# When the first gathered blocks are made: four raw blocks during the load of x, nine beside the terms of the table, and the loop's first loads behind the table's stores

## The chip, the core and the metric

The kernel runs on one core of one Trainium2 chip. The metric is the device time of one execution in microseconds (us). Before the change it is 2218.24 us, the median of 10 runs between 2216.36 and 2223.97.

A core has several engines that run side by side and wait for each other through semaphores: PE multiplies matrices (its weight loads have a row of their own in the profile, PEld), DVE works on vectors element by element, ACT applies functions and copies, POOL is the general engine, which here issues the gathers, and SP issues most other transfers. Transfers are done by 16 DMA engines. [...]

## The reference

One layer of a graph network on 12,500 nodes of 128 features and 212,500 edges that are sorted by their destination `dst`:

```python
h = jnp.maximum(_layernorm(x, axis=-1), 0.0)
q = h @ Wq.T + bq            # per node, 8 heads of 16
v = h @ Wv.T + bv            # per node
k = edge_attr @ Wk.T + bk    # per edge
in_m   = sum(q[src] * k)     # per edge and head
out_m  = sum(q[dst] * k)
diag_m = sum(q[src] * q[dst])
score = (softmax over the edges of each dst of in_m/4, + of out_m/4, + of diag_m/4)
score = score * edge_weight ** lam       # lam = 1
out = x + leaky_relu(segment_sum(score * v[dst]) @ Wo.T + bo)
```

For the change one thing matters: each edge needs the row `q[src]` of an arbitrary node. That row must be gathered, and before it can be gathered from a table the table has to be there.

## The kernel before

**Tiling.** The edges are cut into 415 groups of 512 (four tiles of 128 edges each). Five streams `s` run through the sorted edges at once, 83 blocks `t` each; group `g` is block `g // 5` of stream `g % 5`. The nodes are handled in 25 turns (`GN`) of up to four tiles of 128 nodes.

**The node stage.** A turn normalises its node tiles (statistics on DVE at L869 to L880, the root on ACT at L884, its inverse on DVE at L888 and L889), rectifies them (ACT, L898), turns them with PE and copies the result (L905, L907), multiplies by Wq (L913), adds the bias on DVE (L916) and stores the rows of q to the table `q_table` in memory (SP, L917). The turns are software-pipelined: turn `g` issues the product of its own tiles, the turn of the next and the rectifying of the one after that.

**Gathers.** `gather(g)` issues four indirect transfers on POOL (L683), each of which fetches 128 rows. It cannot take rows from `q_table` before the last of the table is stored. So that POOL need not stand still, the first 13 groups (`RAW`) are gathered from `x` itself; they are called raw blocks. For a raw block the kernel then has to do what a node turn does, on the gathered rows: `raw_measure` (DVE, L957), the sums of a set of up to three blocks, `raw_root` (ACT) and `raw_invert` (DVE), and per block `raw_rectify` (ACT, L972), `raw_turn` (PE L978, ACT L980), `raw_product` (PE L985) and `raw_add` (DVE L989). From group 13 on rows come from `q_table`.

**What sets the order.** Every instruction is pinned in the order in which the program issues it. Between the node turns, `aside(turn)` issues whatever the dictionary `side` holds for that turn; the places are written out by hand. In the kernel before, raw blocks are measured in turns 5 to 7, 12 to 14, 17 to 19, 22, 23, 25 and 26, and block `g` is rectified in turn `9 + 2 * g` for the first seven, in turn `GN + g - 7` for the six others. The dictionary also holds the preparation of the edge tables: casts of the indices to floats (POOL), `edges_1` (POOL, L821), `edges_3` and `edges_5` (DVE), `cuts` (ACT, L835), and `edges_4`, which stores the tables `far_d` and `rel_d` (SP).

**The terms.** For the windows of destination nodes the table also exists as three bf16 terms per value. For the 8 first node turns that the loop needs, `terms_q` makes them after the node stage, in 9 iterations (ACT L933 and L940, DVE L934 and L941), and SP stores them (L943). The raw blocks that are left stand beside these iterations.

**Loads ahead.** `fetch(t)` loads two edge tables of block `t` (`relb`, 630 KB by the profile, L648; `far`, L653) and reads the first node of each window from `places`; `fetch_rows(t)` loads the windows `win` (L665); `fetch_edges(t)` loads 1280 KB of edge features `ea` (L671). `when` (POOL) makes a ruler of expected first nodes, and `near_due` (DVE, L806 to L811) corrects it by the true ones, which gives `places`.

**The loop.** Group `g` of the loop does: products of the window with a one-hot matrix (PE L1224, ACT L1227), the turn and projection of the edge features (PE L1207, L1214, L1216, ACT L1209), three products and a sum on DVE (L1235 to L1238), the one-hot of group `g + 3` (ACT L1201, L1202), and the softmax work of earlier blocks. In iteration `g`, `gather(g + 18)` is held behind PE's products of group `g`, one tile's gather behind each of four places (`behind`). Ahead of the loop 21 groups are gathered. In the first five iterations ACT also issues a large store of blanks each (L1649, 1056 to 1152 KB).

Of the kernel before, what the change touches and what calls it, by code (L numbers as in the profile page):

```python
# [7 lines left out]
F32 = mybir.dt.float32  # L8
# [464 lines left out]
def ordered_path(ctx: ExitStack, tc: tile.TileContext, flag, x, src, dst, edge_attr, edge_weight,  # L473
# [19 lines left out]
    nc = tc.nc  # L493
# [7 lines left out]
    S = 5  # L501
    T = (NB + S - 1) // S
# [17 lines left out]
    START, RATE, NEAR = round(G * BE * N / E), BE * N // E, 90  # L520
# [20 lines left out]
    GN = -(-NI // JN)  # L541
    in_use = sorted((first_use(g), g) for g in range(GN))
    early = [g for t, g in in_use if t < 4]
# [13 lines left out]
    def pin(inst):  # L557

        engine = str(inst.ins.engine)
        if engine in pinned:  # L560
            tc.add_manual_dep(inst.ins, pinned[engine], mybir.DependencyInfo(
                mybir.DependencyClass.NoSync, mybir.DependencyReason.DATA), reason="in order")
        pinned[engine] = inst.ins.name
        return inst
# [15 lines left out]
                   allow_small_or_imprecise_dtypes=True))  # L580
# [29 lines left out]
    bases = consts.tile([1, T, S], I32, name="bases")  # L610
    tops = consts.tile([1, T, S], I32, name="tops")
    heads = consts.tile([1, T, S], I32, name="heads")
    LOOK, QQ, RAW, DRAIN = 18, 20, 13, 12
# [7 lines left out]
    places = consts.tile([1, T, S], I32, name="places")  # L621
# [14 lines left out]
    def block_rows(t):  # L636
        lo = t if t < G else t - 1
        return lo, slice(0, S * G) if t < G else slice(1, S * G + 1)

    def fetch(t):  # L640

        if t >= T:
            return
        at, part = block_rows(t)
        relb = None
        if t < G:
            relb = load.tile([K3, S, BE], BF, name="relb")
            pin(nc.sync.dma_start(relb, rel_d[part].rearrange("(s b) e -> s b e", b=G)  # L648
                                  [None, :, at, :].to_broadcast([K3, S, BE])))
        far = load.tile([R, BE + 1], BF, name="far", bufs=4)  # L650
        lo = t * BE
        of = bass.AP(far_d.tensor, far_d.offset + lo, [[G * BE, S], [0, H3], [1, BE + 1]])
        pin(nc.sync.dma_start(far, of))  # L653
        _, base_v[t] = nc.values_load_multi_w_load_instructions(
            places[0:1, t, 0:S], engines=[mybir.EngineType.SP], min_val=0, max_val=N - 1,
            skip_runtime_bounds_check_because="the indices of nodes are below N")
        st[t] = dict(relb=relb, far=far)
# [10 lines left out]
    def fetch_edges(t):  # L668
        if t < G:
            ea = eas[t] = load.tile([P, S, JN * F], F32, name="ea")  # L670
            pin(nc.sync.dma_start(  # L671
                ea, edge_attr[:end * BE, :].rearrange("(s b p j) f -> p s b (j f)", s=S, b=G, p=P)
                [:, :, t, :]))
# [50 lines left out]
    with tc.tile_pool(name="prep", bufs=1) as prep, \  # L724
# [73 lines left out]
        def of_tile():  # L798
            return prep.tile([P, RC], BF, name="of", tag="of", bufs=2)[:RW]

        def when():
            pin(nc.gpsimd.iota(places, pattern=[[RATE, T], [START, S]], base=0, channel_multiplier=0))

        def near_due():
            offset = prep.tile([1, T, S], F32, name="offset", tag="terms")
            pin(nc.vector.tensor_sub(offset, bases, places))  # L806
            pin(nc.vector.tensor_reduce(found[:, 4:5], offset, AX.XY, ALU.min))
            pin(nc.vector.tensor_reduce(found[:, 5:6], offset, AX.XY, ALU.max))
            pin(nc.vector.tensor_scalar(offset, offset, -float(NEAR), float(NEAR), op0=ALU.max,
                                        op1=ALU.min))  # L810
            pin(nc.vector.tensor_add(places, places, offset))  # L811

        def cast_src():
            pin(nc.gpsimd.tensor_copy(src_f, src_r))
# [78 lines left out]
        def tiles_of(g):  # L893
            return range(g * JN, min(NI, (g + 1) * JN))

        def rectify(g):
            for i in tiles_of(g):
                pin(nc.scalar.activation(xq[:, i, :], xq[:, i, :], AF.Relu, bias=shift[:, i:i + 1],  # L898
                                         scale=inv[:, i:i + 1]))

        def turn_h(g):
            n = len(tiles_of(g))
            h_ps = node_ps.tile([P, JN, P], F32, name="h_ps")
            for b, i in enumerate(tiles_of(g)):
                pin(nc.tensor.transpose(h_ps[:, b, :], xq[:, i, :], ident))  # L905
            hT = hTs[g] = node.tile([P, JN, P], F32, name="hT", bufs=2)
            pin(nc.scalar.copy(hT[:, :n], h_ps[:, :n]))  # L907

        def nodes_q(g):
            n = len(tiles_of(g))  # L910
            q_ps = node_ps.tile([P, JN, F], F32, name="q_ps")
            for b in range(n):
                pin(nc.tensor.matmul(q_ps[:, b, :], hTs[g][:, b, :], wq, start=(b == 0),  # L913
                                     stop=(b == n - 1)))
            q = xq[:, g * JN:g * JN + n, :]
            pin(nc.vector.tensor_add(q, q_ps[:, :n], bq_all[:, None, :].to_broadcast([P, n, F])))  # L916
            pin(nc.sync.dma_start(units(q_table, g * 2, n // 2, F),  # L917
                                  q.rearrange("p (u k) f -> p u (k f)", k=2)))
            del hTs[g]
# [3 lines left out]
        def terms_q(i):  # L923

            if i < len(early):
                g = early[i]
                n = len(tiles_of(g))
                q = xq[:, g * JN:g * JN + n, :]
                q3 = (node.tile([P, JN, 3, F], BF, name="q3", bufs=1) if i % 4 == 1 else
                      prep.tile([P, JN, 3, F], BF, name="q3w", tag="weight") if i % 4 == 0 else  # L930
                      prep.tile([P, JN, 3, F], BF, name="q3o", tag="of", bufs=2))
                q3 = q3s[g] = q3[:, :n]
                pin(nc.scalar.copy(q3[:, :, 0, :], q))  # L933
                pin(nc.vector.tensor_sub(q, q, q3[:, :, 0, :]))  # L934
            if i > 0:
                g = early[i - 1]
                n = len(tiles_of(g))
                q = xq[:, g * JN:g * JN + n, :]
                q3 = q3s.pop(g)
                pin(nc.scalar.copy(q3[:, :, 1, :], q))  # L940
                pin(nc.vector.tensor_sub(q3[:, :, 2, :], q, q3[:, :, 1, :]))  # L941
                lo = g * JN * P
                pin(nc.sync.dma_start(  # L943
                    q3_table[3 * lo:3 * (lo + n * P), :].rearrange("(u p k) f -> p u (k f)", p=P, k=6),
                    q3.rearrange("p (u k) t f -> p u (k t f)", k=2)))
# [48 lines left out]
        def turn_att(a):  # L994
            turn_edges(weight, att_t, [a])

        side = {4: [turn_ws], 5: [cast_src, (gather, 7), cast_dst, (gather, 8)],
                10: [(turn_src, 0)], 11: [(turn_src, 1)], 12: [(turn_src, 2)],
                13: [(turn_src, 3), when, edges_1] + [(gather, g) for g in range(9, RAW)],
                14: [biases], 20: [near_due], 15: [edges_3], 16: [(turn_att, 0), cuts], 17: [(turn_att, 1)],  # L1000
                18: [(turn_att, 2), edges_4], 19: [(turn_att, 3)], 21: [edges_5], 22: [(fetch, 0)]}

        def raw_side(lo, hi, turns):
            for g, turn in zip(range(lo, hi), turns):
                side.setdefault(turn, []).append((raw_measure, lo, hi, g))
            side[turn].append(raw_root)
            side.setdefault(turn + 1, []).append(raw_invert)

        raw_side(0, 3, (5, 6, 7))
        raw_side(3, 6, (12, 13, 14))  # L1010
        raw_side(6, 9, (17, 18, 19))
        raw_side(9, 11, (22, 23))
        raw_side(11, RAW, (GN, GN + 1))
        for g in range(RAW):
            turn = 9 + 2 * g if g < 7 else GN + g - 7
            for k, f in enumerate((raw_rectify, raw_turn, raw_product, raw_add)):
                side.setdefault(turn + k, []).append((f, g))

# [20 lines left out]
        def settle():  # L1039

            while rooted:
                invert(*rooted.pop(0))
# [8 lines left out]
        for g in range(-2, GN):  # L1051
            settle()
            if g + 2 < GN:
                rectify(g + 2)
            if 0 <= g + 1 < GN:
                turn_h(g + 1)
            if g >= 0:
                nodes_q(g)
            ready(g + 4)
            measure(g + 6 + min(max(g, 0), 6))  # L1060
            if g == -2:
                for of in range(7):
                    gather(of)
            aside(g)
            if g == 9:
                fetch_edges(0)
                fetch_few()
        for g in range(RAW, AHEAD):
            gather(g)
        gather_few()  # L1070
        for i in range(len(early) + 1):
            terms_q(i)
            aside(GN + i)
        assert not side

# [115 lines left out]
    with tc.tile_pool(name="work", bufs=2) as work, \  # L1191
# [383 lines left out]

        products = str(mybir.EngineType.PE)
        fetch_rows(0)
        fetch(1)
        fetch_rows(1)
        one_hots(0)  # L1580
        turn(0)
# [168 lines left out]
```

## Time and profile before

| | |
|---|---|
| median of 10 runs | 2218.24 us |
| profiled execution | 2217.78 us |
| its span | 2215.7 us |
| PE busy | 1728.3 us (78%) |
| DVE busy | 2043.0 us (92%) |
| ACT busy | 1369.8 us (62%) |
| POOL busy | 1608.7 us (73%), of it the gathers 1542.3 us |
| first gather from the table | 106.88 us |
| last gather | 2144.56 us |

Starts are in us from the start of the span. A row of the timeline gives the start, the busy time, the engine, the line of the kernel, the operation, what it writes and reads, and in brackets how long the engine was idle before and what ended this. The name of the engine with a q (ACTq, SPq) marks the issue of a transfer, which is not counted as busy. PEclk is the clock that PE was granted, as a share of full speed. A row of the waits gives the engine and its instruction, what it waited for, the sum in us, how often, and the longest. The share of busy time is an average over stages with different limits, so it is read stage by stage. POOL's gathers count as busy for 0.95 us but start 1.26 us apart when nothing holds them, the rest being the issue.

### The profile page before, as it was taken

What the parts mean: (1) busy time and instruction counts of PE and PEld (TensorE: products, weight loads), DVE (VectorE), ACT (ScalarE), POOL (GpSimd) and SP (SyncE); (2) the same over time, 40 slices, a digit from 0 to 9 for tenths busy, and PEclk for the clock granted to TensorE, in tenths of its full rate; (3) what the DMA queues carried; (4) which work ended last, traced back from release to release, by engine and by line L of the source; (5) the groups of instructions that cost most, each with busy time, mean ns of one, the idle gap of its engine ahead of it and who ended that gap; (6) DMA issues with size and microseconds to landing.
All of it is one profiled execution on the core that took longest, in us unless ns stands there. A gap on an engine that the chain in (4) does not pass through costs nothing.

```text
span 2215.7 us, 36271 instructions
## 1 busy us (share of the span) xinstructions
PE 1728.3 (78%) x10744; PEld 1362.6 (61%) x10744; DVE 2043.0 (92%) x2837; ACT 1369.8 (62%) x2517; POOL 1608.7 (73%) x1683
## 2 busy tenths in 40 slices
PE   6767777777777778888878888887888777778775
PEld 4545656665656666666766666665666665556654
DVE  8768999999999999999999999999999999999894
ACT  6756566566666666666666665666666655566661
POOL 7377777777777777777777777777777777777750
PEclk9977888889798888887787888779888988888786
DMA  7676545545555555555455555555455455454531
GB/s 212 199 244 186 162 148 163 181 151 173 168 156 156 178 177 166 154 163 170 141 175 157 150 169 159 147 166 158 150 165 160 149 153 165 149 149 141 159 95 58
DMA packets 321411, 355.65 MB, mean 161 GB/s; under 512 B 135266, under 2 KB 241005, under 8 KB 320896
## 3 DMA queue, kind: packets, MB, share of 16 engines
q1 hardware_dynamic: 250853, 237.91, 34.0%
q0 software_dynamic: 53184, 108.92, 17.3%
q10 hardware_dynamic: 17168, 6.41, 1.2%
q8 instruction: 88, 1.44, 0.3%
q14 instruction: 118, 0.97, 0.1%
HBM read 320.86 MB, written 32.17 MB: 159 GB/s over the span
## 4 chain that ended last, share of the span: by engine, by line
DVE 32%; PE 24%; DMA 21%; ACT 9%; issue 9%; POOL 4%; SPq 0%; DVEq 0%; ACTq 0%; POOLq 0%
DMA qq<-q_table,src_i 20%; DVE lT L1238 10%; PE k_ps L1216 8%; DVE prod L1236 5%; DVE prod L1235 5%; DVE prod L1237 5%; PE w_ps L1388 4%; POOL qq L683 4%; PE eT_ps L1207 3%; PE k_ps L1214 2%; DVE l_ps L1298 2%; PE qd_ps L1224 2%; PE node_ps L1147 1%; ACT relb L1201 1%; ACT eT L1209 1%
## 5 line engine op out<-in xcount | busy, mean ns | idle before, releaser
L683 POOL DMA_INDIRECT qq<-q_table,src_i x1608 | 1542.3, 959 | 513.6 <-issue 220.8
L1238 DVE TENSOR_REDUCE lT<-prod 128x96 f32<-128x1536 f32 x415 | 727.4, 1753 | 14.3
L1216 PEld LDWEIGHTS k_ps<-wk,eT 128*128 128x128 f32 x3320 | 500.9, 231 | 170.7 <-issue 75.9
L1216 PE MATMUL k_ps<-wk,eT 128*128 128x128 f32 x3320 | 593.9, 333 | 12.0 <-ACT eT L1209 11.7
L1209 ACT COPY eT<-eT_ps 128x512 f32<-128x512 f32 x415 | 243.4, 587 | 392.5 <-PE eT_ps L1207 382.2
L1224 PE MATMUL qd_ps<-win,oh 126*128 126x128 bf16 x1660 | 183.0, 240 | 297.8 <-DVE prod L1236 290.4
L1224 PEld LDWEIGHTS <-oh 126*128 126x128 bf16 x1660 | 136.6, 107 | 359.8 <-issue 338.4
L1227 ACT COPY qd<-qd_ps 128x512 f32<-128x512 f32 x415 | 239.3, 577 | 131.4 <-PE qd_ps L1224 109.5
L1207 PE MATMUL eT_ps<-ident,ea 128*128 128x128 f32 x1660 | 311.2, 321 | 2.9 <-DVE qq L989 2.9
L1201 ACT ACTIVATE relb<-relb,before 126x512 bf16<-126x512 bf16 x415 | 301.1, 726 | 0.0
L1236 DVE TENSOR_TENSOR prod<-qq,qd_ps 128x512 f32<-128x512 f32 x412 | 279.9, 679 | 22.9 <-DMA qq<-q_table,src_i 18.7
L1235 DVE TENSOR_TENSOR prod<-qd,k_ps 128x512 f32<-128x512 f32 x415 | 279.5, 673 | 22.1 <-ACT qd L1227 9.2
L1237 DVE TENSOR_TENSOR prod<-qq,k_ps 128x512 f32<-128x512 f32 x412 | 279.6, 679 | 0.0
L1202 ACT ACTIVATE oh<-relb 126x512 bf16<-126x512 bf16 x415 | 261.3, 630 | 16.9 <-DMA q_table<-q3o 3.7
L1207 PEld LDWEIGHTS eT_ps<-ident,ea 128*128 128x128 f32 x1660 | 249.3, 170 | 3.1 <-DVE qq L989 3.1
L1388 PE MATMUL w_ps<-back,sel 128*126 128x144 f32 (+1 forms) x1344 | 207.4, 314 | 44.8 <-ACT sel L1378 37.7
L1388 PEld LDWEIGHTS w_ps<-back,sel 128*126 128x126 f32 (+1 forms) x1344 | 193.9, 211 | 58.4 <-ACT sel L1378 50.3
L1214 PE MATMUL k_ps<-b,ones 3*128 3x512 bf16 x415 | 180.4, 435 | 29.0 <-DVE prod L1237 24.1
L1349 ACT ACTIVATE back<-back 128x480 f32<-128x480 f32 x83 | 50.1, 604 | 190.9 <-DVE back L1348 187.5
L1298 DVE TENSOR_TENSOR_SCAN l_ps<-far,carry,l_ps 120x512 f32<-120x512 bf16 x80 | 102.4, 1280 | 5.2 <-PE l_ps L1258 5.2
L1328 DVE TENSOR_TENSOR_SCAN m<-far,head,l_ps 120x512 f32<-120x512 bf16 x81 | 102.9, 1271 | 0.0
L1340 PE MATMUL m_ps<-ident,m 120*128 120x120 f32 x332 | 77.1, 378 | 24.9 <-DVE m L1328 24.1
(230 smaller groups left out, 1611.3 us busy)
## 6 DMA issues: line engine op xcount, KB each, us to landing
ea<-in_edge_attr_dram SPq DMA_DIRECT2D x83, 1280.0 KB
relb<-rel_d SPq DMA_DIRECT2D x83, 630.0 KB
qq<-q_table,src_i POOLq DMA_INDIRECT x1608
win<-q_table SPq DMA_DIRECT2D x415, 31.5 KB
far<-far_d SPq DMA_DIRECT2D x84, 120.2 KB
q_table<-q SPq DMA_DIRECT2D x18, 384.0 KB
sums<-rows SPq DMA_DIRECT2D x412, 7.9 KB
q_table<-xq SPq DMA_DIRECT2D x24, 256.0 KB
```

The costliest lines, as they stand in the source:

```text
L683: rows = pin(nc.gpsimd.indirect_dma_start(out=qq[:, j, :], out_offset=None, in_=of, in_offset=bass.IndirectOffsetOnAxis(ap=at[:, s, j:j + ...
L1201: pin(nc.scalar.activation(d, d, AF.Abs, bias=before[:K3]))
L1202: pin(nc.scalar.activation(oh, d, AF.Relu, bias=1.0, scale=-1.0))
L1207: pin(nc.tensor.transpose(eT_ps[:, j, :], eas[g // S][:, g % S, j * F:(j + 1) * F], ident))
L1209: pin(nc.scalar.copy(eT, eT_ps))
L1216: pin(nc.tensor.matmul(k_ps[:, j, :], eTs[g][:, j, :], wk, start=False, stop=(j == JN - 1)))
L1224: pin(nc.tensor.matmul(qd_ps[:, j, :], ohs[g][:, j * P:(j + 1) * P], d["win"][:, s, :], start=(j == 0), stop=(j == JN - 1)))
L1235: pin(nc.vector.tensor_mul(prod[:, :, 2, :], qds[g], ks[g]))
L1236: pin(nc.vector.tensor_mul(prod[:, :, 1, :], qqs[g], q_ps[g]))
L1237: pin(nc.vector.tensor_mul(prod[:, :, 0, :], qqs[g], ks[g]))
L1238: pin(nc.vector.tensor_reduce(lTs[t][:, :, s, :], prod.rearrange("p j i (h d) -> p j (i h) d", d=DIM), AX.X, ALU.add))
L1388: pin(nc.tensor.matmul(w_ps[:, i].rearrange("p s c -> p (s c)"), d["sel"][:n, j, lo:lo + 3, :].rearrange("p s w -> p (s w)"), d["back"][:n ...
```

## The change

1. The raw blocks get other places. Blocks 0 to 3 are measured in turns -1, 0, 2 and 3, in two sets of two, and rectified in turns 1, 3, 5 and 7. The others are measured in turns 9 to 11, 17, 18, 22, 23, 25 and 26, and rectified in turns 24 to 32. Turn 25 (`GN`) and those after it are the iterations of the terms, so that nine blocks have their last steps beside the terms, where six had. That loop now has 14 iterations, of which the terms use the first 9.
2. `fetch_edges(0)` moves from behind turn 9, and `fetch(0)` from turn 22, to `GN`, that is behind the last store of `q_table` on SP. `fetch(1)` moves from the start of the loop to `GN + 5`.
3. `when` writes its ruler as floats into the same memory, and `near_due` reads floats; `places` is written as integers as before.
4. Some places move: `cuts` from turn 16 to 18, `edges_4` from 18 to 20 (behind `near_due`), and gather 9 ahead of `edges_1` on POOL.

```diff
+        due = places.bitcast(F32)
+
         def when():
-            pin(nc.gpsimd.iota(places, pattern=[[RATE, T], [START, S]], base=0, channel_multiplier=0))
+            pin(nc.gpsimd.iota(due, pattern=[[RATE, T], [START, S]], base=0, channel_multiplier=0,
+                               allow_small_or_imprecise_dtypes=True))

         def near_due():
             offset = prep.tile([1, T, S], F32, name="offset", tag="terms")
-            pin(nc.vector.tensor_sub(offset, bases, places))
+            pin(nc.vector.tensor_sub(offset, bases, due))
...
-            pin(nc.vector.tensor_add(places, places, offset))
+            pin(nc.vector.tensor_add(places, due, offset))
...
-                13: [(turn_src, 3), when, edges_1] + [(gather, g) for g in range(9, RAW)],
-                14: [biases], 20: [near_due], 15: [edges_3], 16: [(turn_att, 0), cuts], 17: [(turn_att, 1)],
-                18: [(turn_att, 2), edges_4], 19: [(turn_att, 3)], 21: [edges_5], 22: [(fetch, 0)]}
+                13: [(turn_src, 3), when, (gather, 9), edges_1] + [(gather, g) for g in range(10, RAW)],
+                14: [biases], 15: [edges_3], 16: [(turn_att, 0)], 17: [(turn_att, 1)],
+                18: [(turn_att, 2), cuts], 19: [(turn_att, 3)], 20: [near_due, edges_4],
+                21: [edges_5], GN: [(fetch_edges, 0), (fetch, 0)], GN + 5: [(fetch, 1)]}
...
-        raw_side(0, 3, (5, 6, 7))
-        raw_side(3, 6, (12, 13, 14))
-        raw_side(6, 9, (17, 18, 19))
+        raw_side(0, 2, (-1, 0))
+        raw_side(2, 4, (2, 3))
+        raw_side(4, 7, (9, 10, 11))
+        raw_side(7, 9, (17, 18))
         raw_side(9, 11, (22, 23))
         raw_side(11, RAW, (GN, GN + 1))
         for g in range(RAW):
-            turn = 9 + 2 * g if g < 7 else GN + g - 7
+            turn = 1 + 2 * g if g < 4 else GN + g - 5
...
             if g == 9:
-                fetch_edges(0)
                 fetch_few()
...
-        for i in range(len(early) + 1):
-            terms_q(i)
+        for i in range(RAW + 1):
+            if i <= len(early):
+                terms_q(i)
             aside(GN + i)
...
         fetch_rows(0)
-        fetch(1)
         fetch_rows(1)
```

## The prediction

> **What bounds the kernel now.** I read the windows first, to part the span into stages, then POOL's timeline, then ACT's where POOL waits, then the waits.
>
> The windows; columns: window, length, busy time and instructions of PE, PEld, DVE, ACT, POOL, granted clock, DMA share, GB/s.
>
> ```profile
> 101.00:127.00 26.00, 12.70 (x72) 9.71 (x72) 17.28 (x43) 21.84 (x49) 15.55 (x16) 0.87 0.48 153
> 127.00:145.00 18.00, 11.93 (x53) 9.27 (x54) 8.21 (x12) 7.55 (x13) 13.73 (x15) 0.53 0.74 241
> 145.00:170.00 25.00, 14.24 (x83) 10.95 (x81) 15.43 (x19) 10.30 (x18) 19.65 (x21) 0.70 1.06 305
> 300.00:700.00 400.00, 312.68 (x1992) 244.88 (x1993) 381.61 (x485) 252.92 (x450) 303.39 (x317) 0.86 0.54 166
> ```
>
> POOL issues a gather each 1.26 us (400 / 317) in the steady stretch, though only 0.96 of it counts as busy; four to a group, 5.02 us. DVE looks busier, but its waits show who paces it.
>
> POOL's timeline (start, length, instruction, idle before and its releaser):
>
> ```profile
> 106.88 0.95 POOL L683 DMA_INDIRECT qq<-q_table,src_i  x1 [22.08 <-DVE sums L878]
> 177.10 0.95 POOL L683 DMA_INDIRECT qq<-q_table,src_i  x1 [0.55 <-DVE prod L1235]
> 180.18 0.95 POOL L683 DMA_INDIRECT qq<-q_table,src_i  x1 [0.87 <-PE k_ps L1216]
> 191.06 0.95 POOL L683 DMA_INDIRECT qq<-q_table,src_i  x1 [1.15 <-PE qd_ps L1224]
> 2144.56 0.95 POOL L683 DMA_INDIRECT qq<-q_table,src_i  x1 [0.30 <-PE d_ps L1374]
> ```
>
> From 106.88 POOL runs at its pitch. It waits for the loop's front three times, for 0.25 + 0.57 + 0.85 = 1.67 us beyond the usual 0.30, and never after 191.06. The last gather ends at 2145.5, and 70.2 us of fixed tail follow. The waits agree: DVE waits for gathered rows only late, all after 1700.
>
> ```profile
> DVE prod L1236 <- DMA qq<-q_table,src_i: 18.7, 21, 2.3
> ACT raw_inv L884 <- DVE sums L880: 16.6, 5, 7.1
> ```
>
> So the time is the moment at which POOL passes 191.06, plus 2024.6 us that the change does not touch. That moment is set by the front (the products of group 10). A POOL that starts earlier only waits longer.
>
> ACT shows what makes the front late (ACTq rows are DMA issues, in which ACT does nothing else):
>
> ```profile
> 44.45 0.30 ACT L884 ACTIVATE raw_inv<-sums,eps 128x12 f32<-128x12 f32 x1 [7.06 <-DVE sums L880]
> 68.79 0.30 ACT L884 ACTIVATE raw_inv<-sums,eps 128x12 f32<-128x12 f32 x1 [3.93 <-DVE sums L880]
> 130.18 0.63 ACT L1202 ACTIVATE oh<-relb 126x512 bf16<-126x512 bf16 x1 [3.73 <-DMA q_table<-q3o]
> 150.85 3.58 ACTq L1649 DMA_DIRECT2D sums<-jp  x1
> 156.26 3.46 ACTq L1649 DMA_DIRECT2D sums<-jp  x1
> 161.55 6.87 ACTq L1649 DMA_DIRECT2D sums<-jp  x1
> ```
>
> The loop's first one-hot waits for the last q3 store (issued 127.01, landed 130.08). Then the blank stores hold ACT until 168.4, in a window where the DMA engines are full (share 1.06).
>
> **Part 1, four raw blocks in turns 1 to 10.** A block costs ACT 4 x 0.385 + 0.47 = 2.02 us, DVE 0.78 (measure) and 0.60 (add), PE 0.9 + 1.06; a set adds about 0.76 (sums) and 0.33 (invert) on DVE. Up to turn 8 DVE gains 4 x 0.78 + 2 x 1.09 + 4 x 0.60 = 7.7 us and loses three measures and a set, 3.4: +4.3, on an engine busy 9.86 of the 10 us from 30 to 40. ACT gains 8.1 us but has the 7.06 us hole. Bounds: +4.3 if all else overlaps, +12.4 if ACT's 8.1 comes on top. Laying the rows of before end to end in the new order, each after what it needs, I get +6.9 at turn 13's add: DVE's 4.3, and 2.6 for hops between DVE, ACT and PE. I take it, nearer to the lower end because of the hole. Raw rows: blocks 0 to 3 land by the trace at 13.35, 18.47, 22.7 and 30.77, block 3 about when DVE comes to it (30.3 to 31.6). If rows came 4 us later the same laying gives 2.5 more.
>
> **Part 2, turns 13 to 24.** ACT, without a long hole from 69 on, loses blocks 2 to 6 (rectified at 61.2 and later), 5 x 2.02 = 10.1 us, and the hole of 3.93 before 68.79. New holes, where roots at turns 11 and 23 wait for DVE's sums (the second behind near_due 2.6 and edges_5 2.28), and those that vanish, net +2.3 by the same laying. Sum -11.7: the last add moves from 101.1 to about 96.2, and POOL's first table gather from 106.88 to about 100.
>
> **Part 3, the terms stage.** Nine blocks instead of six stand beside the eight terms: 3 x 2.02 = 6.1 us more for ACT, which was idle 26 - 21.84 = 4.2 us there. Bounds +1.9 and +6.1; an iteration with both is 1.54 + 0.47 + 0.51 + 0.52 = 3.05 us with little room, so two short iterations become full ones and I take +4.6, near the upper end. Raw work ends at iteration 10, two beyond the terms; it is a copy, a product and an add by then.
>
> Sum at the last q3 store: +6.9 - 11.7 + 4.6 = -0.2 us, from 127.0 to 126.8. The loop's entry all but stays; what is saved before the table is paid beside the terms.
>
> **Part 4, loads.** ea(0) moves from 63.41, where the window 60 to 85 had share 0.83, to about 97, with relb(0) and far(0) behind the last table store on SP. Issues of 0.65 + 0.41 + 0.85 us; PE needs ea(0) at 127.6 and ACT relb(0) at 125.7, so some 25 us cover them. The two last table stores lose the loads in front of them, but POOL's wait at the front covers that. fetch(1) goes to iteration GN+5, between q3 stores three us apart: its 1.2 us of issue fits, and if it waited, q3 stores 6 to 8 would queue behind it, each us delaying the entry by one. In the loop's start relb(1) and far(1) (0.39 + 0.80 us on SP) no longer stand before win(1) and ea(1), so ea(1) starts 1.2 us earlier out of the full stretch that begins near 142: 0 to -1.2; I take half, -0.6. POOL, 6.9 us ahead, waits for the front instead of gathering, so about five gathers fewer lie in the full stretch: 64 KB each at 305 GB/s, 0.2 us each, 0 to -1.0; I take -1.0, as the blanks drain through what is free. The 1.0 us that ACT waits before the store at 150.85 (for the landing of an earlier blank) may go too, 0 to -1.0, but the queue is bound by its draining: 0.
>
> **Part 5, at nothing.** The float ruler changes readings in near_due's four operations (2.6 us of DVE in turn 20, beside ACT): 0 to -0.4, off the path. POOL's iota (1.38 us as integers) and gather 9, moved ahead of edges_1, stand in POOL's idle 7.54 us before 61.22; without that cover they would cost 2.6. cuts (1.91 us of ACT) and edges_4's three stores come two turns later, still over ten us before fetch(0) reads them.
>
> Row against rule: DVE's two-input operation at 62.48 took 2.37 us until POOL's subtraction ended at 64.82, and 0.17 elsewhere. The Trainium skill, page "SBUF — State Buffer", section "Who interferes with whom", says that a DVE instruction with two SBUF inputs contends with a GpSimd instruction that reads SBUF. By that rule the sums and adds put early into POOL's casts of turn 5 would each wait like this one; by the row that is 2.2 us once more at most.
>
> Total: -0.2 - 0.6 - 1.0 = -1.8. The profiled execution took 2217.78 us (0.46 under the median of 2218.24), so 2216.0 for it, and about **2216.5** for a median.
>
> **Rivals.** About 0.2%, 4.4 us, is what a measurement of this kernel can tell from no change.
> - *Faster, the front gains all.* Part 1 at its lower end (-2.6), part 3 at its lower end (-2.7), ea(1) and ACT's wait whole (-1.6): -8.7, 2209.5; half of that, with the forecast, about 2212. For it: the hole of 7.06 us, and full DMA in the stretch. Against: ACT and DVE alternate in early turns, so holes seldom fill.
> - *Slower, the early turns choke.* DVE has 0.14 us to spare in ten there; if ACT's 8.1 us come on top, the loss at turn 13 is 12.4 instead of 6.9, +5.5, and the terms stage at its upper end +1.5: +5.2 with the rest, 2223.0 for the execution, 2223.5 for a median. It decides once the last q3 store is issued more than 6 us later than 127.0. For it: 44.45 waits for exactly this engine. Against: raw rows are there early for three of four blocks.
> - *It does not do what it says, for the time:* POOL starts earlier and stands at the front, nothing else moves: 2218. This lies within the forecast's case.
>
> A second rule speaks against the change, too. PE's granted clock is 0.53 from 127 to 145 and a group of eight products takes 2.08 us there, 1.16 at full clock. The Trainium skill, "TensorE: Matmul & The Clock Gate", section "Part 1: The HAM clock gate (the "warmup" mystery)", has the clock halved after an idle window of some 3.4 us. By it, raw-only iterations at the end with a sparse PE would leave the loop's first products cold as before, +0; by the row, likewise, 0.92 us a group for three groups are at stake either way.
>
> **How the numbers follow.** Within 0.2% (2213.8 to 2222.7): 0.47, holding the forecast, the third rival, and mild forms of the others; its own range is 2213.8 to 2219.5. Faster 0.30: sums of parts 1 and 3 have a long lower side, and four terms of part 4 point down. Slower 0.23. The ends for 8 in 10: 2209.5, where the faster rival is whole, and 2225.0, the slower rival with 1.5 us for a q3 store behind fetch(1).
>
> **What would show it.** The adds of turns 8, 13, 24 near 50.5, 67 and 96; ACT's hole before 44.45 gone; first table gather near 100; last q3 store near 126.8; POOL waiting some 8 us in all between 140 and 192 where it waited 1.67; its last wait within 2 us of 191; 2024.6 us after it as before. I am wrong if the last q3 store moves by over 3 us, if ACT is free of the blanks well before 166, or if POOL's last wait is no longer at the front of group 10.

## The result and the profile after

The changed kernel takes 2204.77 us (median of 8 runs, 2203.64 to 2208.33), the kernel before 2219.05 us (28 runs). The ratio is 0.9937, with a 95% interval from 0.9929 to 0.9946: 14 us faster, where about 2216.5, too near to the time before to be told from no change, was forecast. The profiled execution took 2205.11 us, its span 2203.2.

POOL's timeline of the changed kernel, at the places that the prediction used (start, length, instruction, idle before):

```profile
102.42 0.94 POOL L683 DMA_INDIRECT qq<-q_table,src_i  x1 [14.42 <-DVE raw_stats L960]
175.36 0.94 POOL L683 DMA_INDIRECT qq<-q_table,src_i  x1 [2.88 <-PE k_ps L1221]
194.33 0.95 POOL L683 DMA_INDIRECT qq<-q_table,src_i  x1 [0.65 <-issue]
2131.73 0.94 POOL L683 DMA_INDIRECT qq<-q_table,src_i  x1 [0.30 <-PE d_ps L1379]
```

POOL starts 4.5 us earlier (102.42 for 106.88) and then waits for the loop's front, 7.5 us in all. Its last wait ends at 194.33, 3.3 us later than the 191.06 of before. So the front lost. Yet the last gather starts at 2131.73, 12.8 us earlier. The gain lies in the steady stretch, where the prediction had nothing to change.

The groups of POOL's instructions in a quiet part of the loop, 940 to 1050 us, say what it is. First before, then after (busy time, then mean ns of one):

```profile
L683 POOL DMA_INDIRECT qq<-q_table,src_i x89 | 84.7, 951 | 27.1 <-issue 12.2 <-DMA qq<-q_table,src_i 6.4 <-PE eT_ps L1207 1.5
```

```profile
L683 POOL DMA_INDIRECT qq<-q_table,src_i x89 | 84.1, 944 | 27.1 <-issue 10.1 <-DMA qq<-q_table,src_i 8.5 <-PE qd_ps L1229 3.0
```

The same gather on the same engine is 8 ns shorter (the medians over the loop are 952 and 944 ns; the gaps of 0.305 us between gathers are equal). From group 29 on POOL never waits longer than this usual gap, before or after, so its pitch sets the time of the loop. A difference of under one per cent in an instruction that runs 1608 times and paces everything is worth more than all the moves of the change together.

The sum, from POOL's rows: group 29's first gather starts at 194.84 before and 198.08 after (+3.24). From there to the last gather it takes 1949.72 and 1933.65 us (-16.07). The end is +0.4. Together -12.4, within rounding the difference of the spans (2215.7 and 2203.2). Of the 16.07, 1543 gathers times 8 ns make 12.3. The rest lies in unusually long gathers: before, 37 took over 1000 ns, 11.2 us above the usual length; after, 30, with 6.9 us.

The stages of the changed kernel (window, length, busy time and count of PE, PEld, DVE, ACT, POOL, clock, DMA share, GB/s):

```profile
101.00:127.00 26.00, 19.18 (x79) 16.48 (x80) 13.97 (x33) 21.35 (x49) 19.32 (x18) 0.50 0.67 213
145.00:170.00 25.00, 16.79 (x99) 13.11 (x97) 18.18 (x20) 11.11 (x19) 17.77 (x19) 0.74 1.02 302
300.00:700.00 400.00, 314.27 (x1993) 247.82 (x1990) 382.32 (x481) 251.44 (x447) 303.00 (x319) 0.85 0.54 165
```

In the terms stage PE's clock is 0.50, where it was 0.87. The full stretch of the DMA engines is nearly as full as before (1.02 for 1.06). In 400 us POOL now issues 319 gathers, where it issued 317.

**What the profile of before had shown already.** The raw gathers, in two windows of the kernel before: 15 to 37 us, and 66 to 84 us.

```profile
L683 POOL DMA_INDIRECT qq<-in_x_dram,raw_i x15 | 14.2, 944 | 4.6 <-issue 4.3 <-DMA src_r<-in_src_dram 0.3
L683 POOL DMA_INDIRECT qq<-in_x_dram,raw_i x15 | 14.3, 952 | 4.6 <-issue 4.6
```

Within one execution the same instruction is 944 ns early and 952 ns later. Between the two windows POOL does something else: two casts, at 38.73 and 45.50, behind which gathers are still short, then the integer ruler at 52.30 and the subtraction `edges_1` at 61.22. The gathers behind these two are long, to the end (median 952).

### The profile page after: what moved, and what is told of

Read it like the earlier page. It is cut to its first block, busy times and chain, and to the rows that moved or that the text cites. A ratio compares the mean times of both kernels' runs of the same rounds, so it can differ in the third digit from the quotient of the medians.

```text
span 2203.2 us, 36272 instructions
## 1 busy us (share of the span) xinstructions
PE 1743.5 (79%) x10744; PEld 1378.7 (63%) x10744; DVE 2040.3 (93%) x2844; ACT 1370.0 (62%) x2518; POOL 1594.9 (72%) x1683
## 4 chain that ended last, share of the span: by engine, by line
DVE 40%; PE 22%; DMA 16%; issue 9%; ACT 8%; POOL 3%; ACTq 1%; DVEq 1%; SPq 0%; POOLq 0%
DMA qq<-q_table,src_i 16%; DVE lT L1243 13%; PE k_ps L1221 7%; DVE prod L1241 6%; DVE prod L1240 6%; DVE prod L1242 6%; PE w_ps L1393 3%; PE eT_ps L1212 3%; POOL qq L683 3%; DVE l_ps L1303 2%; PE k_ps L1219 2%; PE qd_ps L1229 1%; PE node_ps L1152 1%; ACT oh L1207 1%; ACT relb L1206 1%
## 5 line engine op out<-in xcount | busy, mean ns | idle before, releaser
L1241 DVE TENSOR_TENSOR prod<-qq,qd_ps 128x512 f32<-128x512 f32 x412 | 279.8, 679 | 11.2 <-DMA qq<-q_table,src_i 8.9
L1393 PEld LDWEIGHTS w_ps<-back,sel 128*126 128x126 f32 (+1 forms) x1344 | 198.4, 215 | 51.7 <-ACT sel L1383 42.3
```

The lines of the kernel that those rows point to most:

```text
L1241: pin(nc.vector.tensor_mul(prod[:, :, 1, :], qqs[g], q_ps[g]))
L1393: pin(nc.tensor.matmul(w_ps[:, i].rearrange("p s c -> p (s c)"), d["sel"][:n, j, lo:lo + 3, :].rearrange("p s w -> p (s w)"), d["back"][:n ...
```

## The experiments

The experiments test what made the gathers shorter, and what made the front late. The runs fell on several chips. On three of them (the first, third and fourth batch) the kernel before takes 2707 to 2738 us, and the loop waits for something that the trace only calls remote; gathers still start 1.25 us apart where nothing holds them, but POOL does not pace the loop (mean distance 1.49 to 1.51 us from group 29 on). There only the length of a gather is read, and the time says what the moves cost on such a chip. What makes these chips slower was not looked into.

### First batch: which part of the change

```diff
 ruler_alone = before, and
-  iota(places, ...); tensor_sub(offset, bases, places); tensor_add(places, places, offset)
+  iota(due, ...);    tensor_sub(offset, bases, due);    tensor_add(places, due, offset)
 all_but_ruler = after, with these three lines as in before
 extra_int = after, and behind the ruler of floats
+  iota(spare, pattern=[[RATE, T], [START, S]], base=0, channel_multiplier=0)   # int32, read by nothing
 int_first = before, and when() ahead of gather 0 instead of in turn 13
```

Expected of ruler_alone:

> The kernel before with the ruler of floats and nothing else of the change. Theory 1 (the integer ruler slows every gather behind it): gathers take 944 ns all through, where before they took 952 from 64.97 us on; the front is that of before (last wait near 191), and some 1548 gathers behind it save 8 ns each, 12.4 us: 2204 to 2207 us. Theory 2 (where the gathers stand on POOL, gather 9 ahead of edges_1 and the branch behind it, sets their length): 952 ns as before, 2219 us. Theory 3 (the front or the earlier start of POOL made the gain): the time of before.

Expected of all_but_ruler:

> The changed kernel with the integer ruler of before and its readings in near_due; all moves stay. Theory 1: 952 ns from gather 9 on, and the front of the changed kernel, 3.3 us later than before: 2220 to 2224 us, slower than before. Theory 2: 944 ns, about 2205 us. Theory 3: about 2205 us.

Expected of extra_int:

> The changed kernel with one more POOL instruction: behind the ruler of floats an integer ruler of the same pattern is written to a tile that nothing reads. Theory 1: 952 ns from gather 9 on, about 2219 us. Theory 2, and also a theory 1b (what counts is how places itself is written and read): 944 ns, 2205 to 2207 us.

Expected of int_first:

> The kernel before with its integer ruler moved ahead of the first gather on POOL. Theory 1: 952 ns from the first gather on, the time of before, 2219 us. Theory 2: 944 ns up to the branch near 52 us, 952 ns behind it. If the gathers stay at 944 throughout, an integer ruler only matters between gathers: about 2205 us.

Measured, on a chip with 2732.09 us before: ruler_alone 0.9987 (0.9974 to 1.0000), all_but_ruler 1.0039 (1.0026 to 1.0053), extra_int 2744.45 us in one run, int_first 2727.84 us in one run. The gathers' median was 944 to 945 ns in the loop of all four. Theory 1, that any integer ruler slows what comes behind it, had said 952 for the last three: it fell. Theory 2 had said 952 for ruler_alone and for the later gathers of int_first: it fell as well. What was left: none of the four has the integer ruler and the subtraction in a row, as before has. In all_but_ruler and extra_int gather 9 stands between them, in int_first nearly all gathers that were made by then.

### Second batch: the four kernels on a chip that POOL paces

Here before, after, ruler alone and all but the ruler ran beside each other; the ratios are to seven other runs of before (median 2219.82 us).

Expected of before_2 (the kernel before, unchanged):

> The kernel before, unchanged, once more with a profile. In the runs so far gathers took 944 to 945 ns on another chip with either ruler, which is against theory 1 in its plain form. Theory 1c (an integer ruler with POOL's subtraction right behind it and no gather between, an order that only the kernel before has) says 952 ns behind 61 us here. Theory 4 (the 952 ns belong to a chip or to one loading of the program, not to the code) says 944 ns.

Expected of after_2 (the changed kernel, unchanged):

> The changed kernel, unchanged, once more. On a chip like that of the record, theories 1 and 1c say 944 ns and 0.993 to 0.995 of the time before; theory 4 says that the ratio follows the gathers' length: near 1.001 (the front 3 us later) where both kernels gather at the same length.

Expected of ruler_2 (as ruler_alone):

> The ruler of floats alone, once more, for a chip like that of the record. Theories 1 and 1c: 944 ns and 0.992 to 0.995. Theory 2: 952 ns and 1.000. Theory 4: the ratio of no change wherever before gathers at the same length.

Expected of all_but_2 (as all_but_ruler):

> All of the change but the ruler, once more. Theory 1: 952 ns and 1.001 to 1.003. Theory 1c and 2: 944 ns (gathers stand between the integer ruler and the subtraction) and 0.993 to 0.995. Theory 4: the length of the kernel before and 1.001 to 1.002.

| kernel | time, us | ratio (95%) | gather, median ns | group 29 starts | from there to the last gather |
|---|---|---|---|---|---|
| before_2 | 2216.71 (one run) | | 952 | 196.82 | 1947.66 |
| after_2 | 2208.16 | 0.9947 (0.9931 to 0.9964) | 944 | 199.90 | 1934.58 |
| ruler_2 | 2204.26 | 0.9938 (0.9919 to 0.9956) | 944 | 195.28 | 1933.89 |
| all_but_2 | 2207.20 | 0.9940 (0.9918 to 0.9961) | 944 | 199.55 | 1934.20 |

The 952 ns of before came again in another execution, beside kernels with 944 on the same chip, so they belong to the code (theory 4 fell). Theory 3 fell too: ruler_2 has the gain with the front of before. The ruler of floats alone gives the short gathers and the whole gain. So does all the rest without it. One of two things is enough, then: no integer ruler, or gather 9 between the ruler and the subtraction. Both agree with theory 1c, that the pair makes it. The moves of the raw blocks and loads add nothing to the gain that these runs can tell: kernels that have them pass group 29 at 199.55 and 199.90, ruler_2 at 195.28.

### Third batch: the pair by itself

```diff
 gather9_first = before, and
-  13: [(turn_src, 3), when, edges_1] + [(gather, g) for g in range(9, RAW)]
+  13: [(turn_src, 3), when, (gather, 9), edges_1] + [(gather, g) for g in range(10, RAW)]
 int_next = after with the integer ruler, and
-  13: [(turn_src, 3), when, (gather, 9), edges_1] + ...
+  13: [(turn_src, 3), (gather, 9), when, edges_1] + ...
 int_before_cast = before, and
-  5: [cast_src, (gather, 7), cast_dst, (gather, 8)],  13: [(turn_src, 3), when, edges_1] + ...
+  5: [cast_src, (gather, 7), when, cast_dst, (gather, 8)],  13: [(turn_src, 3), edges_1] + ...
```

Expected of gather9_first:

> The kernel before, integer ruler and all, with gather 9 issued between the ruler and POOL's subtraction (edges_1), and nothing else. Theory 1c (integer ruler and subtraction in a row, no gather between): 944 ns throughout, the front of before, 0.992 to 0.995 of the time before on a chip like that of the second batch, 2203 to 2207 us. Theory 5 (some other part of the change lets the integer ruler off, the places of the raw blocks or the loads): 952 ns and 1.000.

Expected of int_next:

> The changed kernel with the integer ruler, issued behind gather 9 and right ahead of the subtraction: all moves of the change, and the pair of before. Theory 1c: 952 ns behind the subtraction, and the front of the changed kernel, 3 to 4 us later than before: 2220 to 2225 us. Theory 5: 944 ns, 2205 to 2209 us.

Expected of int_before_cast:

> The kernel before with its integer ruler ahead of POOL's cast of dst, which runs without any idle time, so that another POOL operation than the subtraction follows it directly and the subtraction has gathers in front. Theory 1c for any operation behind the ruler: 952 ns from 47 us on, 2219 us. Theory 1d (only the subtraction, or only the pair with POOL's idle 7.5 us in it): 944 ns, 2203 to 2207 us.

The chip was one of those that POOL does not pace (2738.41 us before); there the raw gathers ahead of the pair take a median of 947 ns. In gather9_first gathers stay at 947 behind the subtraction and through the loop; the time is 1.0006 (0.9987 to 1.0025). In int_next they go from 947 to 955 at the subtraction and stay; 1.0033 (1.0015 to 1.0052). In int_before_cast (2741.63 us in one run) it happens at the cast, with no idle time in between. POOL's timeline of int_before_cast, around the pair:

```profile
44.74 0.95 POOL L683 DMA_INDIRECT qq<-in_x_dram,raw_i  x1 [0.30 <-issue]
45.71 1.38 POOL L802 IOTA places<- 1x420 int32 x1
47.04 1.88 POOL L817 CAST dst_r<-dst_r 104x2050 f32<-104x2050 int32 x1
49.09 0.98 POOL L683 DMA_INDIRECT qq<-in_x_dram,raw_i  x1 [0.16 <-issue]
```

Its raw gathers from 15 to 37 us, and behind the subtraction from 96 to 115 us, as groups:

```profile
L683 POOL DMA_INDIRECT qq<-in_x_dram,raw_i x15 | 14.2, 946 | 4.6 <-issue 4.6
...
L683 POOL DMA_INDIRECT qq<-in_x_dram,raw_i x15 | 14.4, 958 | 4.6 <-issue 4.6
```

The three gathers between the cast and the subtraction took 955, 955 and 951 ns behind a first one of 980; behind the subtraction it is 958. So the pair with a cast lengthens gathers by some 8 ns, as the pair with the subtraction does (only three gathers show it by itself); behind the subtraction, which here has gathers ahead of it, they are 3 ns longer still, for a reason that no run tells. Theories 1d and 5 fell. And gather9_first shows that one move of a gather, with nothing else of the change, keeps them short. What this move alone gains in time where POOL paces the loop was not measured.

### The loss made again, and the front

```diff
 spread_blanks = after, and
-            if g < S:
-                of = [u for u in range(NU) if g in parts_of(u)]
+            if g % 3 == 0 and g < 3 * S:
+                of = [u for u in range(NU) if g // 3 in parts_of(u)]
-                    sums[g][...]
+                    sums[g // 3][...]
 ruler_loads = ruler_alone, and
-            if g == 9: fetch_edges(0)
-                21: [edges_5], 22: [(fetch, 0)]}
+                21: [edges_5], GN: [(fetch_edges, 0), (fetch, 0)], GN + 5: [(fetch, 1)]}
-        fetch(1)          # at the start of the loop
```

These two and int_next ran first on chips that POOL does not pace. Expected of ruler_loads, ruler_loads_2 and int_next_2 there:

> The kernel before with the ruler of floats and the moved loads (edges and tables of block 0 behind the last table store, of block 1 in iteration 5 of the terms, none at the start of the loop), with the raw blocks where before has them. If the moved raw blocks make the front late (nine iterations of the terms at 3.6 us, with PE at half clock), the last q3 store is issued near 127 to 128 and POOL's last wait stands near 190: 2201 to 2206 us, at or below the ruler alone. If the loads make it late, the last q3 store is near 131 and the time near that of the changed kernel, 2205 to 2210.

> Ruler of floats and moved loads, raw blocks as before, on such a chip. If the nine raw blocks beside the terms make the front late (+5 us at the last q3 store): last q3 store near 127 to 129, POOL's last wait near 190 and 2201 to 2205 us. If the loads do: last q3 store near 131, 2205 to 2209.

> All moves of the change with the integer ruler right ahead of the subtraction, on a chip where POOL paces the loop: 952 ns behind the subtraction. The time is then that of before plus the 2.5 to 4 us of the later front: 2219 to 2224 us, 1.000 to 1.003, some 14 us above the changed kernel. If the moves made the gain, 0.993 to 0.996.

and of spread_blanks:

> The changed kernel with the five blank stores in iterations 0, 3, 6, 9 and 12 of the loop, where they stood in 0 to 4; nothing else. If ACT, held by the issue of these stores, makes the front late, ACT's issues fall below 1 us each, POOL loses most of the 8 to 10 us that it waits between 142 and 197 in the changed kernel, and the time is 2196 to 2201 us on a chip with 2219 before (0.990 to 0.993). If the front is late for another reason (PE at half clock, DVE), the waits stay and the time is that of the changed kernel, 2205 to 2208.

On the times they told nothing of these questions: ruler_loads 1.0023 (1.0007 to 1.0039) and ruler_loads_2 1.0029 (1.0016 to 1.0042), int_next_2 1.0051 (1.0031 to 1.0071), spread_blanks 1.0037 (1.0023 to 1.0051). All of them miss the expected times, which were for a loop that POOL paces; the moves lose 0.2 to 0.5% on such chips, with either length of the gathers. The length in int_next_2 came as expected: 944 ns ahead of the pair, 952 behind it. Then the same kernels ran where POOL paces the loop (2217.26 and 2220.76 us before):

> All moves of the change with the integer ruler right ahead of the subtraction, for a chip where POOL paces the loop. 952 ns behind the subtraction; if the gathers' length alone makes the gain, 1.000 to 1.003, 2219 to 2224 us; if the moves made it, 0.993 to 0.996.

> The changed kernel with the blank stores in iterations 0, 3, 6, 9 and 12, once more, for a chip where POOL paces the loop. If ACT's blocked issues make the front late: POOL waits under 3 us between 142 and 200, 2196 to 2201 us, 0.990 to 0.993. If not: 2205 to 2208 us.

> Ruler of floats and moved loads, raw blocks where before has them, for a chip where POOL paces the loop. If the nine raw blocks beside the terms make the front late: last q3 store near 127 to 129, POOL's last wait near 190, 2201 to 2205 us. If the loads do: last q3 store near 131 and 2205 to 2209 us.

**int_next_3**, with every move of the change and the pair of before: 2220.83 us, 1.0006 (0.9996 to 1.0016). POOL's timeline and the group of raw gathers behind the pair (73.5 to 87.5 us):

```profile
56.40 0.94 POOL L683 DMA_INDIRECT qq<-in_x_dram,raw_i  x1 [0.30 <-issue]
57.36 1.38 POOL L802 IOTA places<- 1x420 int32 x1
69.02 3.60 POOL L821 TENSOR_TENSOR step<-dst_r 104x2049 f32<-104x2049 f32 x1 [10.29 <-PE t_ps L790]
74.05 0.95 POOL L683 DMA_INDIRECT qq<-in_x_dram,raw_i  x1 [0.30 <-issue]
```

```profile
L683 POOL DMA_INDIRECT qq<-in_x_dram,raw_i x12 | 11.4, 953 | 3.5 <-issue 3.4
```

The gain is gone, with 952 ns in the loop and 1949.65 us from group 29 to the last gather. Between this kernel and the changed one lie only the ruler's type, with its readings in `near_due`, and its place. Nearer still is all_but_2: it differs from int_next_3 in nothing but the order of the integer ruler and gather 9. On the same chip all_but_2 took 2207.20 us (beside 2219.82 before) and int_next_3 2220.83 (beside 2217.26); they pass group 29 within 0.6 us of each other (199.55 and 198.98), and from there take 1934.20 and 1949.65 us. That settles where the 14 us come from.

**spread_blanks_2**: 2200.05 us, 0.9915 (0.9897 to 0.9933), 17 us faster than before and the fastest kernel of the study. The three long issues of ACT in the changed kernel are these:

```profile
152.66 5.03 ACTq L1653 DMA_DIRECT2D sums<-jp  x1
159.51 4.06 ACTq L1653 DMA_DIRECT2D sums<-jp  x1
165.39 6.54 ACTq L1653 DMA_DIRECT2D sums<-jp  x1
```

and the five of spread_blanks_2 take 0.4 us each:

```profile
147.39 0.41 ACTq L1653 DMA_DIRECT2D sums<-jp  x1
154.27 0.40 ACTq L1653 DMA_DIRECT2D sums<-jp  x1
170.24 0.38 ACTq L1653 DMA_DIRECT2D sums<-jp  x1
184.53 0.38 ACTq L1653 DMA_DIRECT2D sums<-jp  x1
200.77 0.38 ACTq L1653 DMA_DIRECT2D sums<-jp  x1
```

POOL now waits last at 155.68, 3.5 us in all (under 3 was expected) for 9.5 in after_2, and passes group 29 at 193.10 for 199.90. From 145 to 200 us PE's `k_ps` products wait for ACT's copy `eT` for 10.9 us in after_2, and no longer in spread_blanks_2. So the blank stores did make the front late, as the prediction read them, and POOL's earlier start is paid out only once they are spread. By the waits they did it by holding ACT; but the edit also empties the DMA engines' full stretch (share 0.82 for 0.99 from 145 to 170), and no run parts the two.

**ruler_loads_3**: 2205.29 us, 0.9940 (0.9920 to 0.9959). The last q3 store is issued at 128.27, POOL's last wait ends at 193.02, group 29 starts at 196.77: between ruler_2 (127.15, 195.28) and the kernels with all moves and the blanks where they were (131.6 to 132.1, 198.1 to 199.9). The last q3 store is where it was expected if the raw blocks make the front late, the last wait is later than the 190 expected with it and than ruler_2's 191.53; the time, 2205.3, lies at the border of the two expectations. Taken as they are, these traces give about 1.5 us of the front's lag to the loads and 2 to 3 to the raw blocks. But single executions of one kernel differ by 2 us at this place (194.84 and 196.82 for before), and PE's clock in the terms stage was 0.74 here and 0.85 in ruler_2, so neither share is shown.

## Why the prediction was wrong

**The step that failed is part 5, "at nothing".** It priced the float ruler by its own readings, "0 to -0.4, off the path", and gather 9 ahead of `edges_1` by the idle time that it fills. Each of the two alone takes 8 ns off every later gather, which is 12.3 us from group 29 on. (`near_due`'s operations, which the float ruler was to shorten, take 0.57, 0.58, 0.57, 0.37 and 0.58 us before and after: 0 of the 0.4.) With it falls the sentence "plus 2024.6 us that the change does not touch": from POOL's last wait to the end it is 2008.9 us after. An instruction was priced by what it does and not by what it leaves behind, and a pitch of 1.26 us that had been read from the steady part was taken as a constant of the machine. The two windows of raw gathers in before, 944 and 952 ns, would have raised the question. What the steady stretch lost beyond the 12.3 us lies in long gathers, and no run ties these to the pair.

**What bounds the kernel: right.** POOL paces it, and only the moment at which the front lets POOL pass counts ahead of the steady stretch. The table of the second batch is this sum with the right second term.

**Part 1: right in size early.** Turn 8's add moved from 44.33 to 50.66 (forecast 50.5). ACT's hole of 7.06 us before 44.45 is gone, as foreseen; the longest in its place is 3.86 us, before 26.63. Turn 13's add moved by 8.6 us, to 68.91, where 6.9 had been taken from bounds of 4.3 and 12.4.

**Part 2: too good by about 1.** From turn 13 to the last add the kernel won back 10.8 us, not 11.7. The last add stands at 98.85 instead of 96.2, the first table gather at 102.42 instead of 100.

**Part 3: the right mechanism, mis-sized.** The stage from the last add to the last q3 store grew by 7.4 us (25.9 to 33.3), where +4.6 had been taken and 6.1 was the upper bound. An iteration took 3.6 us instead of 3.05, with PE at half clock throughout: ACT's copy of a turned block waits 0.45 us each time, as here in the changed kernel:

```profile
117.89 0.58 ACT L983 COPY hT<-h_ps 128x512 f32<-128x512 f32 x1 [0.45 <-PE h_ps L981]
118.37 1.65 ACT L975 ACTIVATE qq<-qq,raw_shift,raw_inv 128x128 f32<-128x128 f32 x4
```

The bound was built from ACT's idle time and left PE out. In before_2, with six blocks and PE at half clock too, the stage took 27.7 us, so some 1.8 of the 7.4 go with the clock and 5.6 with the three blocks. So the last q3 store went out at 132.10, 5.1 us later, not 0.2 earlier, which the prediction had named as a sign of being wrong.

**Part 4: about right.** From the last q3 store to POOL's last wait it took 64.05 us before and 62.2 after, -1.8 where -1.6 had been summed; its terms were not tested one by one, so the agreement of the sum may be luck. ACT came free of the blanks at 172.0, 3.6 us later than before. POOL's 7.5 us of waiting match the forecast's "some 8" by luck: POOL was to start 6.9 us earlier and to end its waits where it did before; it started 4.5 us earlier and ended them 3.3 us later.

**The rivals.** The slower one happened in a mild form: the last q3 store went out 5.1 us late, below the 6 that would have decided. The faster one named the front, and the front was late; that the time fell is not its doing. (Half of its gain beyond the forecast would be 2213, not the 2212 given; nothing rests on it.) No rival had the gathers' length, and the range, built from the front alone, ended at 2209.5.

**The moves without the gathers** give 1.0006 in int_next_3, which is where the forecast of no change lay, but by other numbers: the front is 2 to 4 us late (group 29 at 198.98, before at 194.84 and 196.82) where -1.8 was forecast.

## What to carry to other kernels

Where one engine's repeated instruction paces the loop, its length is a quantity to check at the start and at the end of one trace, by the same line and shape; a step of one per cent in it, between two rows of the timeline, is a reason to ask what the engine ran in between. A reorder of one instruction on such an engine can then be worth more than the work that was moved to win time. And a head start for the pacing engine pays only when the next thing in line, here the blank stores on ACT, is moved as well.

## What the runs showed of the hardware

On POOL, an integer iota (the instruction that writes the ruler, 1 x 420) with the subtraction or the cast of a 104-row tile as POOL's next operation, and no gather between, lengthens each indirect gather behind it by 8 ns: 944 to 952 on two chips, 947 to 955 on another, to the last gather. With a float iota of the same pattern, or with one group's gathers in between, it does not. The two float iotas near 160 us in before do not undo it. It is not every such pair: at the start of the program an integer iota is followed by a float iota and fills, ahead of the first gather, and the first gathers are short. What in the engine makes the difference is open; no run tells. That long gathers (over 1000 ns) are also rarer in the kernels with short ones (6.3 to 9.8 us of excess in six traces, 9.5 to 11.4 in three) was seen where POOL paces the loop; on the other chips it was not so (5.7 to 9.1 us in eight traces with short ones, 4.5 to 5.8 in three with long ones), and it is not shown to belong to the pair.

PE's clock in the terms stage differed between two executions of one kernel. The window from 105 to 125 us in before, in before_2 and in the changed kernel (columns as above):

```profile
105.00:125.00 20.00, 11.38 (x68) 9.16 (x68) 11.55 (x27) 17.21 (x39) 14.16 (x14) 0.86 0.44 140
105.00:125.00 20.00, 13.66 (x58) 11.99 (x58) 9.96 (x24) 15.92 (x37) 13.06 (x12) 0.50 0.43 139
105.00:125.00 20.00, 14.59 (x60) 12.65 (x60) 10.48 (x26) 15.98 (x36) 15.74 (x15) 0.50 0.63 199
```

With six raw blocks it was also 0.85 in ruler_2 and 0.74 in ruler_loads_3, which passed from half to full clock near 116 us. The iterations of before took 3.06 us and those of before_2 3.6, and the last q3 store went out at 127.01 and 129.74. With nine blocks the clock was 0.50 in four traces on chips that POOL paces and 0.59 in the fifth. The Trainium skill, "TensorE: Matmul & The Clock Gate", section "Part 1: The HAM clock gate (the "warmup" mystery)", has the clock full after some 3.4 us of sustained work. No stretch here is that long: PE works for 2.9 us and has a hole of 0.67 us in each 3.6. One such stretch was followed by full clock in before, where the next eight products take 1.16 us; in the changed kernel none of six was, and they take 2.08. First before, then the changed kernel:

```profile
107.77 2.08 PE L985 MATMUL q_ps<-wq,hT 128*128 128x128 f32 x8 [3.79 <-ACT hT L980]
109.64 1.06 PE L978 MATMUL h_ps<-ident,qq 128*128 128x128 f32 x4
111.37 1.16 PE L985 MATMUL q_ps<-wq,hT 128*128 128x128 f32 x8 [0.68 <-ACT hT L980]
```

```profile
111.31 2.08 PE L988 MATMUL q_ps<-wq,hT 128*128 128x128 f32 x8 [0.67 <-ACT hT L983]
```

How work with holes counts for the clock is left open by these runs.

Chips differ: the same kernel before took 2217 to 2221 us in three batches and 2707 to 2738 us in three others, where kernels with moves of the change lost 0.2 to 0.5% and shorter gathers brought little (0.9987 for the ruler alone).
